# Second half's variances computed by ScalarE in the query stage, five other sums placed elsewhere, last blocks sent in halves by two queues: one transformer block on Trainium2

## The chip, the cores and the metric

The kernel runs on one core of a Trainium2 chip. A core has five engines that work side by side, each with a stream of instructions of its own that it carries out in order: TensorE (PE, matrix products, into the eight banks of the accumulator memory PSUM), VectorE (DVE), ScalarE (ACT), GpSimd (POOL) and SyncE (SP, which here only issues transfers). Sixteen DMA engines move data between device memory and the on-chip memory SBUF. Engines wait for one another by semaphores.

The metric is the device time of one execution in microseconds (us). The change is judged by the median of several runs against runs of the kernel before on the same chip.

## What is computed

The reference adds a masked cross-attention with 32 heads in 8 groups to `x`, and then a gated feed-forward block (FFN). All data are fp32; `x` is 16 x 128 x 1024, so 2048 rows of 1024.

```python
def _layernorm(x, axis=-1, eps=1e-05):
    m = jnp.mean(x, axis=axis, keepdims=True)
    v = jnp.var(x, axis=axis, keepdims=True)
    return (x - m) / jnp.sqrt(v + eps)
...
    def _L0_xattn_ref(q, k, v, w_q, w_k, w_v, w_out, mask):
...
        query = q @ w_q.T
        key = k @ w_k.T
        value = v @ w_v.T
...
        scores = jnp.einsum('bghnd,bgsd->bghns', query, key) / D_HEAD ** 0.5
        scores = jnp.where(mask, scores, jnp.finfo(scores.dtype).min)
        attention = jax.nn.softmax(scores, axis=-1)
        out = jnp.einsum('bghns,bgsd->bghnd', attention, value)
        out = out.transpose(0, 3, 1, 2, 4).reshape(b, n, D_MODEL)
        return out @ w_out.T

    def _L0_ffn_ref(x, w12, b12, w3, b3):
...
        x12 = jnp.einsum('bsk,mk->bsm', x, w12) + b12
        x1, x2 = jnp.split(x12, 2, axis=-1)
        x4 = jax.nn.silu(x1) * x2
        return jnp.einsum('bsm,nm->bsn', x4, w3) + b3
    x = x + _L0_xattn_ref(_layernorm(x, axis=-1), ctx_4096, ctx_4096, L0_xattn_w_q, L0_xattn_w_k, L0_xattn_w_v, L0_xattn_w_out, mask_SxS2_bk0)
    x = x + _L0_ffn_ref(_layernorm(x, axis=-1), L0_ffn_w12, L0_ffn_b12, L0_ffn_w3, L0_ffn_b3)
    return x
```

## The kernel before

**Products in seven instead of eight.** The large matrix products use a Strassen-like scheme: a product of 2 x 2 blocks is made from seven block products, of sums and differences of the blocks. The function `seven` runs the seven in a given order (`INNER` is 1, 5, 6, 7, 2, 3, 4) and calls a `hook(j)` after the j-th of them. One product is two instructions of 128 x 512 results per chunk; a chunk is about 0.86 us of TensorE. For the queries and for the FFN's first layer two levels are nested: an *outer* product `i` of seven is one step, and in it the *inner* products `k` of seven run. The last layer (w3) uses a scheme of 26 products, `bilinear`, for four groups `k` = 0 to 3.

The price of it is sums on the other engines. `q_outer_right(i, h, c)` makes an outer sum of the transposed `x` for product `i` (`Y`, L499, on VectorE or GpSimd); `q_inner_right(i, k)` makes from it the inner sum that product `k` needs (`Y_T`, L509, VectorE, 128 x 1024). Likewise `outer_right` (L1066 and following, on the normalised activations `xnT`) and `inner_right` (`X_T`, L1086) for the FFN. The weights' sums (`QI`, L303) run on GpSimd. Results of PSUM banks are combined on VectorE (`Q_u`, `F_u`, L287 and L290, `QUr` at L600 and L602, `M` at L1176), with a first copy by ScalarE (`Q_p`, `F_p`, L284).

**Stages**, in us of the profiled span: keys and values of the first half (0 to 65); query steps 0 to 9 (65 to 186; a step is 14 products of about 0.86 us, 12.0 us; step 3 begins at 95.4, 4 at 107.4, 5 at 119.4, 6 at 131.4, 7 at 145.6, 8 at 157.6, 9 at 169.6); attention for the first eight tiles of 128 rows (T = 0), with the remaining query steps and the second half's keys and values in between (186 to 343); attention for the other eight (T = 1) with the output projection (343 to 633); the FFN's first layer (633 to 978); w3 and the final sums (978 to 1160).

**Order.** In the query steps and in the FFN the program order of TensorE, VectorE, ScalarE, GpSimd and SP is the order in which the work is written (a manual schedule). What is to run beside the products is put into a plan: `q_at(n, j, fn, ...)` has `fn` run at hook j of query step n, `at(n, j, fn, ...)` at hook j of FFN step n. In the attention stages only TensorE's order is written by hand (`tick`, `soon` and the stream mix the attention of a tile with the products of other stages); for the other engines the scheduler of the language orders the instructions by its own estimate. Tiles come from pools: 44 buffers of 128 x 1024 (`unit`, also used by `load`), 14 of 128 x 512 (`temp`), eight banks. A buffer is passed on when its last reader is done; a load into it waits for that on its queue.

**The norm of the attention.** The layer norm's mean is taken out of the products in another way; what each tile `t` needs is 1/std. For tiles 0 to 7 (`mr[0]`) ScalarE makes the variance in the query steps: `load_xs(t)` at hook 1 of step t + 1, `q_squares(t)` at hook 2 of step t + 2 (two passes over 128 x 1024 with a sum, L626 and L628, a small negation between them, L627), then `inv_std`. For tiles 8 to 15 (`mr[1]`) VectorE does it by statistics instructions in the attention of T = 0: `mean_var` (L204 to L211) has two `bn_stats` (L208), one aggregation (L210) and a copy (L211) for a tile; loads and calls stand in the hook of `seven_round` (L733 to L736). `inv_std` (L213 to L224) is six small operations on GpSimd and two on ScalarE. The values are used from `scores` on, where `s` (L760, VectorE) scales the scores by 1/std and adds the mask; then the maximum (L763), the exponentials on ScalarE (`p`, L769), the reciprocal of the sum (L775, VectorE), the scaling of `p` (L778, GpSimd), the transposes (`pt`, TensorE L784) and their copies (L787, L789). `vt` (L426) are TensorE's transposes of the second half's values.

**Other work that the change touches.** `sums_left7(1, 0)` makes the sums of the key weights for the second half's keys, eight GpSimd additions of 128 x 256 (`A_S`, L303); the scheduler of T = 0 places them. `wo_T` and `wo` (L242) are sums of the output projection's weights by VectorE and GpSimd, `ctx_T` and `ctx` (L700) of the second half's context. `made(i, blocks, sums)` plans the four outer sums (`blocks`) and the inner ones of FFN product i; `quiet(n, c)` gives the first c of the hook positions (n, 7), (n+1, 1), (n+1, 2). For w3, `direct` (L1283 to L1288) adds a finished PSUM block or an intermediate sum into the rows `x1_in`; if it is the last term of a block of 128 x 512 (`final`), the block is sent to `out` by SP's queue.

Of the kernel before, what the change touches and what calls it, by code (L numbers as in the profile page):

```python
# [14 lines left out]
ALU = mybir.AluOpType  # L15
# [113 lines left out]
def xattn_ffn_kernel(  # L129
# [75 lines left out]
    def mean_var(xt, dst, name):  # L205
        st = small.tile([P, 2, nc.vector.BN_STATS_DIM], F32, tag="st", name=f"st_{name}")
        for h in range(2):
            nc.vector.bn_stats(st[:, h, :], xt[:, ts(h, 512)])  # L208
        mv = small.tile([P, 2], F32, tag="mv", name=f"mv_{name}")
        nc.vector.bn_aggr(mv, st)  # L210
        nc.vector.tensor_copy(dst, mv)  # L211
# [204 lines left out]
    def load_xs(t):  # L416
        xs[t] = load(x[t], [D], f"xs_{t}")

    def stats(t):
        mean_var(xs.pop(t), mr[t // NT][:, :, t % NT], f"a{t}")  # L420

    def turn_V(T, c, r, t):

        pt = bank(f"vt_{T}_{c}_{r}").rearrange("p (t k) -> p t k", t=4)
# [189 lines left out]
            *((INNER,) if n < AHEAD else ((1, 6, 5, 7, 2, 3, 4), nc.vector.tensor_copy)),  # L614
        )

    def q_stats(t):
        stats(t)
        if t % NT == NT - 1:
            inv_std(mr[t // NT], f"a{t // NT}")  # L620

    def q_squares(t):

        xt = xs.pop(t)
        less = mr[0][:, 0, t : t + 1]
        nc.scalar.activation(xt, xt, AF.Identity, accum_out=less)  # L626
        nc.scalar.mul(less, less, -1.0 / D)  # L627
        nc.scalar.activation(xt, xt, AF.Square, bias=less, accum_out=mr[0][:, 1, t : t + 1])  # L628
        if t == NT - 1:
            nc.gpsimd.tensor_scalar(mr[0][:, 1, :], mr[0][:, 1, :], 1.0 / D, None, ALU.mult)  # L630
            inv_std(mr[0], "a0")

    def q_plans():
        for n, (g, i) in enumerate(Q_STEPS):
            if i > 2:
                q_at(n - 2, 3, q_load_left, g, i)
            for e, k in enumerate((1, 5, 6, 7, 3)):
                q_at(n - 1, 3 + e if n else min(5 + e // 2, 7), q_inner_left, g, i, k)
            if i in (1, 2, 5, 3):
                q_at(n - 1, 6 if n else 7, q_hold, g, i)  # L640
            if i == 1:
                q_at(g - 1, 7, q_keep_left, g, 4)
                q_at(g - 1, 7, q_outer_left, g)
                q_at(g, 7, q_keep_left, g, 3, 6)
                q_at(g + 1, 2, q_keep_left, g, 5, 7)
                q_at(n + 1, 2, q_store, g, i, "U")
            if i == 2:
                q_at(n + 1, 2, q_gather, g, 2, "U")
                q_at(n + 2, 3, q_final, g, 2, 0, 0)
            if i == 6:  # L650
                q_at(n - 2, 4, q_fetch, g, "U")
                q_at(n + 1, 2, q_store, g, "u", "V")
            if i == 7:
                q_at(n + 1, 2, q_store, g, "u", "W")
            if i == 4:
                q_at(n, 7, q_stay, g, "u", 1)
            if i == 5:
                q_at(n + 1, 3, q_gather, g, "V", 5)
                q_at(n + 1, 3, q_gather, g, "W", 5)
                q_at(n + 1, 4, q_given, g, "W", 1)  # L660
            if i == 3:
                q_at(*((n + 1, 3) if g == 0 else (n, 7)), q_gather, g, "V", 3)
                q_at(n, 7, q_given, g, "V", 0)
        for e, (K, C) in enumerate(((0, 0), (1, 0), (1, 1), (0, 1))):
            for f, (h, c) in enumerate(((0, 0), (0, 1), (1, 1), (1, 0))):
                when = ((-1, 3 + (f + 1) // 2), (0, 1 + f), (0, 5 + f // 2), (1, 2 + f))[e]
                q_at(*when, load_xq, K, C, h, c)
        for i, hcs, ks in (
            (1, [(-1, 5)] * 4, ((-1, 6), (-1, 6), (-1, 7), (0, 1))),
            (2, [(0, 6)] * 4, ((0, 7), (1, 1), (1, 2), (1, 7))),  # L670
            (5, [(2, 1), (2, 2), (2, 7), (3, 1)], ((8, 7), (9, 1), (9, 2), (9, 7))),
            (6, [(2, 7), (3, 1), (3, 3), (3, 3)], ((3, 5), (3, 6), (3, 7), (4, 1))),
            (7, [(4, 5), (5, 1), (5, 2), (5, 5)], ((5, 2), (5, 7), (6, 1), (6, 2))),
            (4, [(6, 5), (7, 1), (7, 2), (7, 5)], ((7, 2), (7, 7), (8, 1), (8, 2))),
            (3, [(4, 4)] * 4, ((4, 4), (5, 4), (8, 4), (8, 6))),
        ):
            for when, hc in zip(hcs, ((0, 0), (0, 1), (1, 1), (1, 0))):
                q_at(*when, q_outer_right, i, *hc)
            for when, k in zip(ks, (5, 6, 7, 4)):
                q_at(*when, q_inner_right, i, k)  # L680
        for t in range(NT):
            q_at(t + 1, 1, load_xs, t)
            q_at(t + 2, 2, q_squares, t)
        for m in (0, 1, 4, 5):
            q_at(8, 1 + m, q_home, 0, m)
        q_at(11, 3, load_left7, 1)
        for j, e in ((1, 0), (1, 5), (2, 1), (4, 3)):
            q_at(12, j, lambda e=e: ctx_work[1][e][1]())
        for when, i, e in (
            ((12, 6), 5, 0), ((12, 7), 5, 1), ((13, 2), 6, 0), ((13, 4), 6, 1), ((13, 5), 7, 0), ((13, 7), 7, 1),  # L690
        ):
            q_at(*when, ctx_sum, i, e)
        q_at(13, 3, sums_left7, 1, 0)

    def ctx_sum(i, e):

# [19 lines left out]
    def seven_round(T, k, R):  # L716
        def done(rc, s, ps):
            r, c = rc
            dst = temp([512], f"vT_{T}_{c}_{r}") if k else key_home(T, c, r)
            if s is None:  # L720
                nc.scalar.copy(dst, ps)
            else:
                nc.vector.tensor_add(dst, s, ps)
            if k:
                soon(3, turn_V(T, c, r, dst))

        def hook(j):
            tick()
            if (T, k, j) == (1, 0, 4):
                sums_left7(1, 1)  # L730
            if (T, k) == (1, 0) and j < 3:
                ctx_sum(4, j - 1)
            if T == 1 and j < 5:  # L733
                load_xs(NT + 4 * k + j - 1)
            if T == 1 and j > 2 and j < 7:
                q_stats(NT + 4 * k + j - 3)  # L736
            transition(T, k, j)

        yield from seven(left7.pop((T, k)), R, f"Q7_{T}_{k}", done, hook, (1, 2, 5, 6, 7, 3, 4))
# [506 lines left out]
    made(1, [(-1, 1)] * 4, sums((-1, 2), (-1, 3), (-1, 4), (-1, 5)))  # L1246
    made(2, [(0, 1)] * 4, sums(*(quiet(n, 1)[0] for n in range(4))))
    made(3, [(4, 1)] * 4, sums(*(quiet(n, 1)[0] for n in range(4, 8))))
    made(5, quiet(7, 3) + quiet(8, 1), sums(*(quiet(n, 2)[1] for n in range(11, 15))))
    made(6, quiet(8, 3)[1:] + quiet(9, 2), sums(quiet(9, 3)[2], *quiet(10, 3)))  # L1250
    made(7, quiet(15, 2) + quiet(16, 2), sums(*quiet(17, 2), *quiet(18, 2)))
    made(4, [quiet(n, 1)[0] for n in range(11, 15)], sums(*(quiet(n, 1)[0] for n in range(19, 23))))
# [29 lines left out]
    def summed(k):  # L1282
        def direct(n, t, s, in_psum, final):  # L1283
            i, c = divmod(n, 2)
            part = x1_in[k][i][:, ts(c, 512)]
            put(nc.vector if in_psum else nc.gpsimd, part, part, "+" if s > 0 else "-", t)
            if final:
                nc.sync.dma_start(out[4 * COLS[k] + i][:, ts(c, 512)], part)  # L1288
# [124 lines left out]
```

## Time and profile before

| What | us |
| --- | --- |
| median of 3 runs | 1160.79 (1159.80, 1162.68, 1160.79) |
| the profiled execution | 1162.42 |
| its span (first to last instruction) | 1160.6 |
| TensorE busy | 1141.1 (98%) |
| VectorE busy | 848.8 (73%) |
| GpSimd busy | 653.0 (56%) |
| ScalarE busy | 395.4 (34%) |
| mean granted clock of TensorE | 0.997 of full speed |

The profiled execution lies 0.14% above the median and within the runs shown; 1.8 us of it are outside the span. In the profile, `L426` is line 426 of the kernel, `vt<-ident,vT` says that the tile `vt` is written from `ident` and `vT`, and a group's numbers are instructions, busy time and the mean of one in ns. A wait is put down to the instruction that ended it: `PE vt L426 <- ACT p L769` means that TensorE's instruction of line 426 waited for ScalarE's of line 769. The *chain of waits* goes back from the last instruction to what released it, and so on. In the windows, `PEclk` is the clock granted to TensorE, 1.00 being full speed.

### The profile page before, as it was taken

The page shows a single profiled execution, that of the slowest core. Times are in us where ns is not written, and L with a number is a line of the kernel's source. Part 1 is how long each engine was busy: PE and PEld are TensorE (multiplying, and loading weights), DVE is VectorE, ACT ScalarE, POOL GpSimd, SP SyncE. Part 2 cuts the span into 40 slices and gives each one's busy share as a digit, 9 for nine tenths or more (in the row PEclk, how much of TensorE's full clock was granted, in tenths as well). Part 3 has the DMA queues.
Part 4 walks back from the last instruction along what each step waited for, and adds up shares of the span by engine and source line. Part 5 has one row for each costly group of instructions (what it writes and reads, how often), then busy time and mean ns, then how long its engine had stood idle before and what let it go on. Part 6 is the DMA issues. An engine that isn't in the chain of part 4 may idle for free.

```text
span 1160.6 us, 13625 instructions
## 1 busy us (share of the span) xinstructions
PE 1141.1 (98%) x4232; PEld 534.2 (46%) x4232; DVE 848.8 (73%) x1179; ACT 395.4 (34%) x1429; POOL 653.0 (56%) x591
## 2 busy tenths in 40 slices
PE   9999999999989999999999999999999999999998
PEld 4444444445445554545454544444444444444443
DVE  4577988798977778778546456757777887979772
ACT  1222223657557576666361321210011022111211
POOL 5669935786567456547533359822523342648465
PEclk9999999999989999999999999999999999999999
DMA  9699674954254330332584889858734878282511
GB/s 364 251 368 348 227 265 144 211 154 153 91 200 181 128 128 37 128 128 91 200 306 165 315 334 326 237 199 259 176 121 159 212 197 272 91 270 82 173 73 73
DMA packets 70233, 227.42 MB, mean 196 GB/s; under 512 B 7824, under 2 KB 7824, under 8 KB 70160
## 3 DMA queue, kind: packets, MB, share of 16 engines
q1 hardware_dynamic: 62672, 199.81, 46.7%
q0 software_dynamic: 6624, 24.12, 11.2%
q10 hardware_dynamic: 864, 2.62, 0.6%
q8 instruction: 34, 0.56, 0.2%
q14 instruction: 39, 0.32, 0.1%
HBM read 139.49 MB, written 79.69 MB: 189 GB/s over the span
## 4 chain that ended last, share of the span: by engine, by line
PE 91%; DVE 4%; ACT 2%; issue 1%; DMA 1%; POOL 1%; SPq 0%; ACTq 0%; POOLq 0%; DVEq 0%
PE F_b L199 28%; PE Q_b L199 21%; PE O_b L199 15%; PE G_b L199 15%; PE pt L784 4%; PE s L751 3%; PE o L799 2%; ACT p L769 2%; PE xt L899 1%; DVE ctx_T L700 1%; DVE s L760 0%; DVE xnT L1066 0%; DVE Y_T L509 0%; DMA xnr<-xn_dram 0%; PE vt L426 0%
## 5 line engine op out<-in xcount | busy, mean ns | idle before, releaser
L769 ACT ACTIVATE p<-s,nmax 128x128 f32<-128x128 f32 x512 | 181.8, 406 | 125.7 <-DVE nmax L763 114.8
L778 POOL TENSOR_TENSOR p<-p,inv 128x512 f32<-128x512 f32 x128 | 136.4, 1098 | 138.4 <-DVE inv L775 121.1
L199 PE MATMUL F_b<-X_T,L 128*128 128x512 f32 x304 | 135.7, 592 | 0.0
L769 ACT ACTIVATION_READ_ACCUMULATOR p<-s,nmax 128x1 f32 x512 | 125.5, 245 | 0.0
L199 PE MATMUL G_b<-w_R,A_L 128*128 128x512 f32 x256 | 114.5, 592 | 0.0
L760 DVE SCALAR_TENSOR_TENSOR s<-s,mr,drop 128x512 f32<-128x512 f32 x128 | 90.3, 750 | 28.8 <-PE s L751 28.6
L784 PEld LDWEIGHTS pt<-ident,p 128*128 128x128 f32 x512 | 63.6, 142 | 70.0 <-issue 63.5
L199 PEld LDWEIGHTS F_b<-X_T,L 128*128 128x128 f32 x304 | 57.4, 190 | 70.8 <-issue 68.6
L763 DVE TENSOR_REDUCE nmax<-s 128x4 f32<-128x512 f32 x128 | 81.7, 679 | 0.0
L284 ACT COPY F_p<-F_b 128x512 f32<-128x512 f32 x28 | 16.4, 586 | 188.3 <-PE F_b L199 188.3
L784 PE MATMUL pt<-ident,p 128*128 128x128 f32 x512 | 77.3, 274 | 1.5 <-issue 1.5
L303 POOL TENSOR_TENSOR x<-x,G_n 128x512 f32<-128x512 f32 x36 | 52.8, 1491 | 46.3 <-DVE G_n L366 29.4
L384 ACT COPY G_c<-G_b 128x512 f32<-128x512 f32 x52 | 30.5, 586 | 140.7 <-PE G_b L199 137.3
L199 PEld LDWEIGHTS G_b<-w_R,A_L 128*128 128x128 f32 x256 | 48.6, 190 | 61.3 <-issue 59.3
L1176 DVE TENSOR_TENSOR M<-F_u,F_b 128x512 f32<-128x512 f32 x57 | 39.0, 685 | 46.3 <-PE F_b L199 42.8
L303 POOL TENSOR_TENSOR x<-x,G_c 128x512 f32<-128x512 f32 x36 | 54.8, 1538 | 31.9 <-DMA x<-x_dram 13.0
L199 PE MATMUL Q_b<-Y_T,QI 128*128 128x512 f32 x136 | 62.4, 594 | 1.9 <-DVE Y_T L509 1.9
L199 PE MATMUL O_b<-wo_T,O_S 128*128 128x512 f32 x128 | 63.3, 603 | 0.0
L199 PE MATMUL O_b<-wo,O_S 128*128 128x512 f32 x128 | 62.5, 602 | 0.0
L199 PE MATMUL F_b<-xnT,L 128*128 128x512 f32 x128 | 60.9, 593 | 0.0
L199 PE MATMUL O_b<-wo,OTr 128*128 128x512 f32 x112 | 56.0, 603 | 0.0
L287 DVE TENSOR_TENSOR F_u<-F_b,F_p 128x512 f32<-128x512 f32 x28 | 19.3, 691 | 45.2 <-PE F_b L199 41.5
(244 smaller groups left out, 2265.9 us busy)
## 6 DMA issues: line engine op xcount, KB each, us to landing
w<-in_w_dram SPq DMA_DIRECT2D x36, 512.0 KB, 6.3
xq<-in_xT_dram SPq DMA_DIRECT2D x16, 512.0 KB, 9.8
xs<-in_x_dram SPq DMA_DIRECT2D x16, 512.0 KB, 6.8
xp<-in_x_dram SPq DMA_DIRECT2D x16, 512.0 KB, 6.6
x_dram<-xp SPq DMA_DIRECT2D x16, 512.0 KB, 2.8
xn_dram<-xn SPq DMA_DIRECT2D x16, 512.0 KB, 2.9
xnr<-xn_dram SPq DMA_DIRECT2D x16, 512.0 KB, 5.7
h<-hT_dram SPq DMA_DIRECT2D x16, 512.0 KB, 6.0
```

Source lines behind the costliest of these rows:

```text
L199: nc.tensor.matmul(ps, lhsT, rhs, start=start and i == 0, stop=stop and i == len(pairs) - 1, skip_group_check=True,)
L287: nc.vector.tensor_add(u1, banks[6], p1)
L303: (eng.tensor_add if op == "+" else eng.tensor_sub)(out, a, b)
L384: nc.scalar.copy(t, ps)
L751: nc.tensor.matmul(ps[gl][:, j, :], QT[T, gh * HPG + j][rows, c, toks], KT[T, c][rows, gh, toks], start=True, stop=True,)
L760: nc.vector.scalar_tensor_tensor(s, s, rstd, drop.unsqueeze(1).to_broadcast([P, HPG, S]), ALU.mult, ALU.add,)
L763: nc.vector.tensor_reduce(nmax[:, e], s, AX.X, ALU.max, negate=True)
L769: nc.scalar.activation(p[:, j, :], ps[gl][:, j, :], AF.Exp, bias=nmax[:, e, j : j + 1], accum_out=total[:, e, j : j + 1],)
L778: nc.gpsimd.tensor_mul(p, p, inv[:, e].unsqueeze(2).to_broadcast([P, HPG, S]))
L784: nc.tensor.transpose(pt[:, j, :], p[:, j, :], ident)
L799: nc.tensor.matmul(o[ds(gl * DH, DH), :, :], V[T, c][:, i, ts(gh * GL + gl, DH)], pTs[gl], start=True, stop=True,)
L1176: nc.vector.tensor_add(dst, s, ps)
```

## The change

It has five parts. (1) The second half's variances: `stats`, `q_stats` and their loads in the hook of `seven_round` go; `q_squares` serves both halves. For tile 8 + t the load stands at hook 3 (even t) or 5 (odd t) of query step 3 + t//2, and the squares one step and one hook later. The last calls `inv_std(mr[1])`. (2) Inner sums of the queries: that of k = 6 for outer product 7 from hook 7 to hook 4 of step 5; for outer product 3, k = 6 from (5, 4) to (8, 3), k = 7 from (8, 4) to (8, 5), k = 4 from (8, 6) to (9, 4). (3) `sums_left7(1, 0)` from (13, 3) to (12, 2). (4) Two of the four outer sums of FFN product 5: from (7, 7), (8, 1), (8, 2), (8, 7) to (7, 7), (8, 1), (8, 7), (9, 1). (5) In the last group of w3 (`k == 3`) a block that ends with a PSUM term (there are four) is added in two halves of 256 columns, and each is sent as soon as it is added, the first by SP's queue, the second by ScalarE's.

TensorE's instructions and their order are the same in both kernels. VectorE has 16 `bn_stats`, 8 aggregations and 8 copies less and 4 additions more (each of half the size); ScalarE has 24 activations and 4 transfers more. In the scheduled attention stage of T = 0, GpSimd's eight `A_S` sums come ahead of the `p` scaling of tile 1, one of two `wo` sums of GpSimd comes between the two pairs of `p` scalings that it used to follow, and one `wo_T` sum of VectorE takes the place of two `bn_stats` some 8 us earlier.

```diff
--- before.py
+++ after.py
@@ -416,9 +416,6 @@
     def load_xs(t):
         xs[t] = load(x[t], [D], f"xs_{t}")
 
-    def stats(t):
-        mean_var(xs.pop(t), mr[t // NT][:, :, t % NT], f"a{t}")
-
     def turn_V(T, c, r, t):
 
         pt = bank(f"vt_{T}_{c}_{r}").rearrange("p (t k) -> p t k", t=4)
@@ -614,21 +611,17 @@
             *((INNER,) if n < AHEAD else ((1, 6, 5, 7, 2, 3, 4), nc.vector.tensor_copy)),
         )
 
-    def q_stats(t):
-        stats(t)
-        if t % NT == NT - 1:
-            inv_std(mr[t // NT], f"a{t // NT}")
-
     def q_squares(t):
 
         xt = xs.pop(t)
-        less = mr[0][:, 0, t : t + 1]
+        T, e = divmod(t, NT)
+        less = mr[T][:, 0, e : e + 1]
         nc.scalar.activation(xt, xt, AF.Identity, accum_out=less)
         nc.scalar.mul(less, less, -1.0 / D)
-        nc.scalar.activation(xt, xt, AF.Square, bias=less, accum_out=mr[0][:, 1, t : t + 1])
-        if t == NT - 1:
-            nc.gpsimd.tensor_scalar(mr[0][:, 1, :], mr[0][:, 1, :], 1.0 / D, None, ALU.mult)
-            inv_std(mr[0], "a0")
+        nc.scalar.activation(xt, xt, AF.Square, bias=less, accum_out=mr[T][:, 1, e : e + 1])
+        if e == NT - 1:
+            nc.gpsimd.tensor_scalar(mr[T][:, 1, :], mr[T][:, 1, :], 1.0 / D, None, ALU.mult)
+            inv_std(mr[T], f"a{T}")
 
     def q_plans():
         for n, (g, i) in enumerate(Q_STEPS):
@@ -670,9 +663,9 @@
             (2, [(0, 6)] * 4, ((0, 7), (1, 1), (1, 2), (1, 7))),
             (5, [(2, 1), (2, 2), (2, 7), (3, 1)], ((8, 7), (9, 1), (9, 2), (9, 7))),
             (6, [(2, 7), (3, 1), (3, 3), (3, 3)], ((3, 5), (3, 6), (3, 7), (4, 1))),
-            (7, [(4, 5), (5, 1), (5, 2), (5, 5)], ((5, 2), (5, 7), (6, 1), (6, 2))),
+            (7, [(4, 5), (5, 1), (5, 2), (5, 5)], ((5, 2), (5, 4), (6, 1), (6, 2))),
             (4, [(6, 5), (7, 1), (7, 2), (7, 5)], ((7, 2), (7, 7), (8, 1), (8, 2))),
-            (3, [(4, 4)] * 4, ((4, 4), (5, 4), (8, 4), (8, 6))),
+            (3, [(4, 4)] * 4, ((4, 4), (8, 3), (8, 5), (9, 4))),
         ):
             for when, hc in zip(hcs, ((0, 0), (0, 1), (1, 1), (1, 0))):
                 q_at(*when, q_outer_right, i, *hc)
@@ -681,6 +674,8 @@
         for t in range(NT):
             q_at(t + 1, 1, load_xs, t)
             q_at(t + 2, 2, q_squares, t)
+            q_at(3 + t // 2, 3 + t % 2 * 2, load_xs, NT + t)
+            q_at(4 + t // 2, 4 + t % 2 * 2, q_squares, NT + t)
         for m in (0, 1, 4, 5):
             q_at(8, 1 + m, q_home, 0, m)
         q_at(11, 3, load_left7, 1)
@@ -690,7 +685,7 @@
             ((12, 6), 5, 0), ((12, 7), 5, 1), ((13, 2), 6, 0), ((13, 4), 6, 1), ((13, 5), 7, 0), ((13, 7), 7, 1),
         ):
             q_at(*when, ctx_sum, i, e)
-        q_at(13, 3, sums_left7, 1, 0)
+        q_at(12, 2, sums_left7, 1, 0)
 
     def ctx_sum(i, e):
 
@@ -730,10 +725,6 @@
                 sums_left7(1, 1)
             if (T, k) == (1, 0) and j < 3:
                 ctx_sum(4, j - 1)
-            if T == 1 and j < 5:
-                load_xs(NT + 4 * k + j - 1)
-            if T == 1 and j > 2 and j < 7:
-                q_stats(NT + 4 * k + j - 3)
             transition(T, k, j)
 
         yield from seven(left7.pop((T, k)), R, f"Q7_{T}_{k}", done, hook, (1, 2, 5, 6, 7, 3, 4))
@@ -1246,7 +1237,7 @@
     made(1, [(-1, 1)] * 4, sums((-1, 2), (-1, 3), (-1, 4), (-1, 5)))
     made(2, [(0, 1)] * 4, sums(*(quiet(n, 1)[0] for n in range(4))))
     made(3, [(4, 1)] * 4, sums(*(quiet(n, 1)[0] for n in range(4, 8))))
-    made(5, quiet(7, 3) + quiet(8, 1), sums(*(quiet(n, 2)[1] for n in range(11, 15))))
+    made(5, quiet(7, 2) + quiet(8, 2), sums(*(quiet(n, 2)[1] for n in range(11, 15))))
     made(6, quiet(8, 3)[1:] + quiet(9, 2), sums(quiet(9, 3)[2], *quiet(10, 3)))
     made(7, quiet(15, 2) + quiet(16, 2), sums(*quiet(17, 2), *quiet(18, 2)))
     made(4, [quiet(n, 1)[0] for n in range(11, 15)], sums(*(quiet(n, 1)[0] for n in range(19, 23))))
@@ -1283,6 +1274,11 @@
         def direct(n, t, s, in_psum, final):
             i, c = divmod(n, 2)
             part = x1_in[k][i][:, ts(c, 512)]
+            if final and in_psum and k == 3:
+                for h, queue in enumerate((nc.sync, nc.scalar)):
+                    put(nc.vector, part[:, ts(h, 256)], part[:, ts(h, 256)], "+" if s > 0 else "-", t[:, ts(h, 256)])
+                    queue.dma_start(out[4 * COLS[k] + i][:, ds(512 * c + 256 * h, 256)], part[:, ts(h, 256)])
+                return
             put(nc.vector if in_psum else nc.gpsimd, part, part, "+" if s > 0 else "-", t)
             if final:
                 nc.sync.dma_start(out[4 * COLS[k] + i][:, ts(c, 512)], part)
```

## The prediction

> **What bounds the kernel now.** I read the page's busy times first, then TensorE's waits, the chain of waits around each, and last the windows.
>
> ```profile
> PE 1141.1 (98%) x4232; PEld 534.2 (46%) x4232; DVE 848.8 (73%) x1179; ACT 395.4 (34%) x1429; POOL 653.0 (56%) x591
> ...
> PE 91%; DVE 4%; ACT 2%; issue 1%; DMA 1%; POOL 1%; SPq 0%; ACTq 0%; POOLq 0%; DVEq 0%
> ```
>
> TensorE works 1141.1 of 1160.6 us. The edits leave its instructions and their order alone, so a gain can only come out of the other 19.5 us or out of time at a lowered clock. TensorE's own waits (total, times, longest) show where:
>
> ```profile
> PE vt L426 <- ACT p L769: 5.3, 1, 5.3
> PE Q_b L199 <- DVE Y_T L509: 1.9, 1, 1.9
> ...
> PE F_b L199 <- DVE M L1176: 1.2, 1, 1.2
> ...
> PE s L751 <- DVE QM L606: 0.9, 1, 0.9
> ```
>
> The longest, followed back through the chain (start, us, what):
>
> ```profile
> 313.20 1.15 DVE st_a L208 x2
> 314.35 1.14 DVE wo_T L242
> 315.49 0.12 DVE mv_a L210
> 315.61 1.86 DVE wo_T L242
> 317.47 2.23 DVE mr L211
> 319.70 0.59 DVE st_a L208
> 320.30 1.32 DVE s L760 x2
> ...
> 323.88 1.11 PE vt L426 x4
> ```
>
> TensorE ran out of work at 318.53 and resumed at 323.88. ScalarE's exponentials are what it waits for, but they were waiting for `s` at 320.30, and VectorE had spent 313.20 to 320.30 on the second half's variances (L208, L210, L211) and two sums `wo_T`. The idle time also lowered the clock (windows: length, busy us of PE, PEld, DVE, ACT, POOL, then PEclk):
>
> ```profile
> 315.00:320.00 5.00, 3.53 (x36) 1.27 (x28) 5.00 (x5) 0.00 (x0) 5.00 (x3) 1.00 0.00 0
> 320.00:325.00 5.00, 1.12 (x5) 1.12 (x6) 5.00 (x9) 2.68 (x16) 1.98 (x1) 0.62 0.01 2
> 325.00:330.00 5.00, 5.00 (x16) 2.62 (x16) 3.61 (x9) 4.72 (x23) 3.32 (x5) 0.70 0.75 220
> ```
>
> At half clock a mean of 0.62 means 0.76 of the 5 us at half, and 0.70 means 0.60: 3.8 + 3.0 = 6.8 us, from about 321.2 to 328.0. TensorE worked 4.1 us of it (323.88 to 328.0) at half speed, so it lost 2.05 us beside the idle 5.34. The wait costs 7.4 us.
>
> **The change, part by part.**
>
> *Variances.* Out go 16 `bn_stats` (0.68 us each), 8 aggregations (0.20) and 8 copies (0.18, one 2.31): 10.9 + 1.6 + 3.6 = 16.1 us of VectorE. Around the wait it loses 313.20–314.35, 315.49–315.61 and 317.47–320.30. What is late next is the pair of `wo_T` sums. Alone they take 1.22 each: `s` starts at 313.2 + 2.44 = 315.6. Beside a GpSimd sum of two SBUF operands the same VectorE form takes 1.74 to 3.37 (L509), and GpSimd here has `p` (1.04, 2.02) and its own `wo` sums (3.33, 2.34), one of which now comes earlier: 313.2 + 1.94 + 3.3 = 318.4 at worst. I take the middle, 317.0. From `s` to `vt` it was 323.88 − 320.22 = 3.66, so `vt` starts at 320.7 (319.3 to 322.1) against 318.53: a wait of 2.2 (0.8 to 3.5). The clock fell 321.2 − 318.53 = 2.7 us into the wait, and the 1.91 us wait at 135 left it at 1.00, so 2.2 us should leave it whole. Gain 5.34 − 2.2 + 2.05 = **5.2**; from 5.34 − 3.5 = 1.8 (clock still lost) to 5.34 − 0.8 + 2.05 = 6.6.
>
> The Trainium skill, "TensorE: Matmul & The Clock Gate", Part 1, says that the clock falls after an idle window of about 3.4 us that runs free of the program. By that rule a wait between 2.7 and 3.4 us might keep its clock, and the gain would be up to 2 us larger than the row makes it there; for a wait of 2.2 both give 5.2.
>
> The work goes to ScalarE: 8 × (1.06 + 0.19 + 0.20 + 1.15 + 0.19 = 2.79) = 22.3 us in query steps 4 to 7, two tiles a step, which had one. ScalarE's busy time there is:
>
> ```profile
> 119.40:131.40 12.00, 12.00 (x29) 5.32 (x28) 11.83 (x15) 3.08 (x6) 10.90 (x7) 1.00 0.73 271
> 131.40:145.60 14.20, 12.29 (x30) 5.22 (x29) 13.39 (x13) 3.08 (x6) 14.12 (x8) 1.00 0.42 153
> 145.60:157.60 12.00, 12.00 (x29) 5.31 (x28) 10.10 (x11) 3.08 (x6) 9.63 (x9) 1.00 0.60 218
> ```
>
> 3.08 + 5.6 = 8.7 of 12.0 fits, so nothing on the path; uncovered it would be 22.3. Eight loads of 512 KB move with it, from 250–330 to steps 3 to 6. SP issues them in order, and DMA's share in steps 2 to 4 is over 1.0 (1.02, 1.05, 1.04 in windows cut by step). Loads behind them are `QL`, needed by GpSimd's `QI`: in step 4 `QL` was issued at 109.89, landed at 120.12, and `QI` took it at 121.6. `QI` is 3 us or more ahead of TensorE. A buffer of 44 is owned by somebody else until that work ends, so some of the loads wait on SP for a square or a write (a write of `Q_dram` landed at 117.74), but SP idles from 112.8 to 122.2. I take 0; the other end stands as a rival. GpSimd's six small operations of `inv_std` come at 156 to 159, ahead of `QI` that is needed at 166: 0.
>
> *Query sums.* The wait at 135.02:
>
> ```profile
> 132.35 1.14 DVE QUr L602
> 133.48 3.31 DVE Y_T L509
> ```
>
> `Y_T` (k=6 of i=7) is made just ahead of its product, with GpSimd's `xq` sum (2.81 us from 132.89) beside it. Three hooks earlier it starts near 127.9 and takes the 1.74 us of the `Y_T` that stood there. Behind it k=7's sum (1.74 at 136.71) starts at 133.41 and must be done by 136.6: alone at 134.6, beside `xq` at 136.8, so 0 to 0.3 us remain. Gain 1.91 minus 0.2 = **1.7** (1.0 if the earlier sum delays step 5's `QUr` chain, to 1.9). Steps 8 and 9 take the three moved sums of i=3, 1.2 each; in step 9 VectorE has idles of 0.25 + 1.03 + 0.30 = 1.6 ahead of the chain that starts at 183.17 (`Y_T`, then `s`): 0, at most 1.2 without that cover.
>
> *Left sums.* Eight GpSimd sums (5.65 us) move from 241–249 to 221.8, where GpSimd idles till 225.16. They hold `p` of 225.16 back by 2.4 us, which TensorE turns only at 236. They free GpSimd at 241–245.7, where `p` waited; then `ctx` of 249.08 is over sooner and `ctx_T`, 4.00 us at 252.51 beside two-operand GpSimd work, comes nearer its 1.22, and `QM` behind it at 256.44 ends the wait of 0.94. I take half of it, **0.5** (0 to 0.94 + 0.45 for the small wait at 249.48).
>
> *FFN sums.* Ahead of the wait at 746.48:
>
> ```profile
> 736.71 1.14 DVE X_T L1086
> 737.85 3.35 DVE xnT L1066 x2
> 741.20 0.11 issue
> 741.31 1.74 DVE xnT L1066
> ...
> 746.96 0.69 DVE M L1176
> ```
>
> Three `xnT` sums hold `F_u` to 742.98; with two it starts at 741.3, 1.7 earlier, more than the wait of 1.21. The other two are then both in step 9, where `F_u` started at 754.93, right after `X` sums. They were 1.26 at 750.31 and one more of 1.26 to 1.74 joins; of that VectorE's idle in 748.2–750.3 covers most. Gain **1.2** (0.2 if 1 us of it comes back there, to 1.21).
>
> *Tail.* The last add took 0.69 (128x512), issue at 1157.36, landing 1159.40, end 1160.62. Halves take 0.42 each (128x256): the second ends 0.15 later, both transfers are half as large. 256 KB is a small part of the 2.04 us, since four such transfers just before land 0.6 to 1.2 us apart. Gain **0.1** (−0.3 to +0.4).
>
> The Trainium skill, "DMA: Bandwidth & Descriptors", in "Issuing engines are not separate DMA queues" and "Anatomy of one DMA", speaks against this edit: queues share the 16 engines, and about 2 us of a transfer is fixed. By it the halves would bring nothing but the issue time, 0; by the rows 0.1.
>
> *Sum:* 5.2 + 1.7 + 0.5 + 1.2 + 0.1 = 8.7 us. The profiled execution took 1162.4 (span 1160.6 and 1.8 around it), so the same execution would take 1153.7. The median of the runs shown, 1160.8, is 1.6 lower: **1152.1**. All upper ends together give 6.6 + 1.9 + 1.4 + 1.2 + 0.4 = 11.5, thus 1149.3.
>
> **Rivals.**
>
> *`wo_T` takes the place of the statistics* (0.18). GpSimd's work of 313–322 stays beside `wo_T`, both run near 3 us, and `s` comes at 318.4: that part brings 1.8 only. For it: `mr`'s copy of two numbers took 2.31 while GpSimd's `wo` sum ran from 316.35. Against: `wo_T` took 1.22 and 1.94 in just this neighbourhood. 8.7 − 3.4 = 5.3: 1155.5.
>
> *The moved work stalls where it is put* (0.13): besides, FFN's wait moves to 755, the left sums hold `p` back until it shows, `Y_T` keeps 0.9. All lower ends: 1.8 + 1.0 + 0 + 0.2 − 0.3 = 2.7: 1158.1. Also what it would be if the change did not do what it says at 318. Against: each of the three places has the idle time given above.
>
> *Slower: ScalarE waits in order for a late load* (0.11). The square stands ahead of the next step's copy `Q_p` in ScalarE's order. If its tile has not landed, `Q_p` and the two products' banks behind it wait. A tile has 12.9 us from its hook to its square (a step and one hook of 0.86). A load that waits 5.9 us on SP (the longest wait of that queue for TensorE at 95–119) and takes 13.8 (the longest there, issued at 96.22) is 6.8 late. TensorE goes on for 8 banks × 0.86 = 6.9 minus one being filled and the copy (0.86 + 0.59), 5.4 us. It decides from there: 6.8 costs 1.4 once; 7.6 us late in each of four steps, 4 × 2.2 = 8.8, eats up the gain; 9 us late, with waits past the 2.7 us and one clock loss, is 4 × 3.6 + 2.05 = 16.4: 1168.5. For it: DMA at 1.05, and eight more transfers. Against: its share falls to 0.73 and 0.42 in steps 4 and 5, where most of the new loads are.
>
> **How the numbers follow.** Likeliest 0.58, at 1152.1, with an own range of 1149.3 to 1155.5; rivals 0.18, 0.13 and 0.11. The range takes in the first three cases with the bounds of their parts, and leaves out little but the slower rival: 1148.5 to 1160.0. The runs shown lie 2.9 us apart, 0.25%, so 0.3% or 3.5 us is about what is told from no change. Faster than 1157.3: the first two cases, 0.76. Within: the third, 0.13. Slower than 1164.3: 0.11, the last.
>
> **What would show it.** Right: no wait of TensorE over 3 us after 300, PEclk 1.00 at 320–330, `s` at L760 before 318.5; no wait for `Y_T` near 135; none for `M` near 746 or 757; ScalarE busy near 8.7 us in steps 4 to 7 and TensorE 12.0 of 12.0 in each. Wrong: `vt` still waiting 3.5 us or more behind `wo_T`; a wait of Q_b for Q_u or `QI` between 95 and 186; a new wait near 236 for `p`.

## The result: slower by 0.4%

| Kernel | median, us | runs | ratio to the kernel before, 95% interval |
| --- | --- | --- | --- |
| before | 1160.09 | 10 (1158.75 to 1162.68) | |
| changed | 1165.38 | 10 (1163.11 to 1167.85) | 1.0040 [1.0028, 1.0052] |

5.3 us were lost where 8.7 were forecast as a gain. The page of the changed kernel's profiled execution (1164.81 us, span 1163.0), its engines' busy times:

```profile
PE 1141.6 (98%) x4232; PEld 533.5 (46%) x4232; DVE 838.9 (72%) x1151; ACT 415.2 (36%) x1469; POOL 652.8 (56%) x592
```

VectorE has 9.9 us less (16.1 had been counted out), ScalarE 19.8 more, and TensorE's work is what it was. So the time went into waits again. TensorE's waits in the changed kernel (total, times, longest; line numbers have moved, L423 is `vt`, L760 the exponentials, L775 the transposes `pt`, L1167 `M`):

```profile
PE Q_b L199 <- POOL QI L303: 4.4, 2, 4.1
PE vt L423 <- ACT p L760: 2.4, 1, 2.4
PE pt L775 <- ACT p L760: 1.6, 1, 1.6
...
PE Q_b L199 <- DVE xq L506: 1.4, 1, 1.4
...
PE F_b L199 <- DVE M L1167: 0.4, 1, 0.4
```

The waits that were aimed at did shrink: `vt` from 5.3 to 2.4, the one for `Y_T` from 1.9 to 0.3, `M` from 1.2 to 0.4. Three new ones have come: `QI` (4.1 at 127.5), `xq` (1.4 at 141.9) and `pt` (1.6 at 242.7). Two of these are among the signs of being wrong that the prediction named: a wait for `QI` between 95 and 186, and one for `p`, which it put near 236.

How far the same TensorE instruction is behind the kernel before, from the start times of the two traces, gives each place its price (us; negative is earlier):

| Place (us in the changed kernel) | what | difference |
| --- | --- | --- |
| start to 124 | run-to-run, see the last section | −0.75 |
| 124 to 135 | wait for `QI`, and a stretch at half clock behind it | +5.8 |
| 140 | `Y_T` no longer waited for | −2.0 |
| 142 to 166 | `xq` and `Y_T` late behind the first wait | +2.0 |
| 243 to 251 | `pt`, and `Q_b` and `s` behind it | +3.3 |
| 264 | `s` no longer waits for `QM` | −1.2 |
| 325 to 352 | `vt`: shorter wait, one stretch at half clock instead of two | −3.5 |
| 750 | FFN (0.8 of it the wait for `M`) | −1.0 |
| end | tail, from the end of the last product | −0.3 |
| sum | | +2.4 |

The sum is that of the two spans (1163.0 and 1160.6). The medians lie further apart because the profiled execution of the kernel before was 2.3 above its median and that of the changed kernel 0.6 below.

Where the `QI` wait comes from is seen on GpSimd. Its timeline in the changed kernel (start, duration, line, operation, and in brackets the idle time before and what ended it):

```profile
107.36 0.86 POOL L570 DMA_DIRECT2D QM<-QU_dram  x1 [0.63 <-DVE QM L603]
118.90 0.72 POOL L303 TENSOR_TENSOR QI<-QL 128x256 f32<-128x256 f32 x1 [10.68 <-DMA Q_dram<-QM]
...
124.41 4.66 POOL L496 TENSOR_TENSOR xq<-xq,xq 128x1024 f32<-128x1024 f32 x2
129.04 1.70 POOL L303 TENSOR_TENSOR QI<-QL 128x256 f32<-128x256 f32 x1
130.82 0.73 POOL L303 TENSOR_TENSOR QI<-QI,QL 128x256 f32<-128x256 f32 x1
```

GpSimd stands still for 10.7 us, and not for an input: it waits until the transfer `Q_dram<-QM` has landed. It *writes* `QI`, and the buffer that `QI` got is the one that `QM` is still being sent out of. Behind that, all of GpSimd's order is late; TensorE goes on at 131.6, when the two `QI` sums of 129.04 and 130.82 are done. In the kernel before, GpSimd's waits for `QI` from 92 to 134 were these:

```profile
POOL QI L303 <- DMA QL<-QS_dram: 1.0, 1, 1.0
```

The wait also cost clock; windows of the changed kernel (length, busy PE, PEld, DVE, ACT, POOL, then PEclk, DMA share, GB/s):

```profile
124.00:129.00 5.00, 3.51 (x8) 1.25 (x7) 2.21 (x1) 4.20 (x10) 5.00 (x3) 1.00 0.99 375
129.00:134.00 5.00, 2.37 (x3) 1.18 (x4) 4.93 (x5) 0.00 (x0) 4.92 (x5) 0.71 1.02 382
```

ScalarE, which had got the squares, idles from 129 to 134: it isn't what is late. DMA is full in both windows, so two explanations were open: the buffer, or the eight more transfers.

### The profile page after: what moved, and what is told of

Its sections match the earlier page's. It is cut to its first block, busy times and chain, and to the rows that moved or that the text cites. A ratio compares the mean times of both kernels' runs of the same rounds, so it can differ in the third digit from the quotient of the medians.

```text
span 1163.0 us, 13650 instructions
## 1 busy us (share of the span) xinstructions
PE 1141.6 (98%) x4232; PEld 533.5 (46%) x4232; DVE 838.9 (72%) x1151; ACT 415.2 (36%) x1469; POOL 652.8 (56%) x592
## 4 chain that ended last, share of the span: by engine, by line
PE 87%; DVE 5%; DMA 3%; ACT 2%; issue 2%; POOL 1%; DVEq 0%; ACTq 0%; POOLq 0%; SPq 0%
PE F_b L199 28%; PE Q_b L199 18%; PE G_b L199 15%; PE O_b L199 15%; PE pt L775 4%; PE s L742 3%; PE o L790 2%; ACT p L760 2%; DMA Q_dram<-QM 1%; DVE s L751 1%; DMA xs<-in_x_dram 1%; DVE nmax L754 1%; DVE xp L870 1%; PE xt L890 1%; DVE ctx_T L695 1%
## 5 line engine op out<-in xcount | busy, mean ns | idle before, releaser
L760 ACT ACTIVATE p<-s,nmax 128x128 f32<-128x128 f32 x512 | 181.8, 406 | 124.4 <-DVE nmax L754 108.5
L769 POOL TENSOR_TENSOR p<-p,inv 128x512 f32<-128x512 f32 x128 | 139.0, 1124 | 136.3 <-DVE inv L766 117.9
L760 ACT ACTIVATION_READ_ACCUMULATOR p<-s,nmax 128x1 f32 x512 | 125.3, 245 | 0.0
L775 PEld LDWEIGHTS pt<-ident,p 128*128 128x128 f32 x512 | 63.8, 142 | 71.8 <-issue 62.9
L775 PE MATMUL pt<-ident,p 128*128 128x128 f32 x512 | 77.6, 275 | 3.1 <-ACT p L760 1.6
L1167 DVE TENSOR_TENSOR M<-F_u,F_b 128x512 f32<-128x512 f32 x57 | 39.0, 685 | 45.7 <-PE F_b L199 41.9
L303 POOL TENSOR_TENSOR x<-x,G_c 128x512 f32<-128x512 f32 x36 | 52.0, 1462 | 31.7 <-DMA x<-x_dram 12.9
```

The source lines that it names most:

```text
L303: (eng.tensor_add if op == "+" else eng.tensor_sub)(out, a, b)
L760: nc.scalar.activation(p[:, j, :], ps[gl][:, j, :], AF.Exp, bias=nmax[:, e, j : j + 1], accum_out=total[:, e, j : j + 1],)
L769: nc.gpsimd.tensor_mul(p, p, inv[:, e].unsqueeze(2).to_broadcast([P, HPG, S]))
L775: nc.tensor.transpose(pt[:, j, :], p[:, j, :], ident)
```

## The experiments

Which buffer a tile gets is fixed when the program is built: the pool hands out one of 44 by what it reckons to be free first. The addresses in the compiled programs show which tile had the buffer before; the waits in the profiles agree with them. For the second group's `QI` of product 6 (query step 5):

| Kernel | the `QI` buffer's last owner | tile 11's load (SP) |
| --- | --- | --- |
| before | a query weight, long done | none |
| changed | `QM`, being written to `Q_dram` | another `QM`, being written |
| `qi_same_buffer` | `QM`, being written to `Q_dram` | another `QM`, being written |
| `qi_free_buffer` | tile 8, until its squares | tile 9 |
| `qi_free_sp_waits` | tile 2, until its squares | `QM`, being written |
| `late_two_steps`, `late_three_steps`, `traffic` | a query weight, long done | none in step 4 |

**The first part alone** (`var_only`): the kernel before with the loads and squares of part 1 as the change has them, parts 2 to 5 left out.

```diff
+            q_at(3 + t // 2, 3 + t % 2 * 2, load_xs, NT + t)
+            q_at(4 + t // 2, 4 + t % 2 * 2, q_squares, NT + t)
...
-            if T == 1 and j < 5:
-                load_xs(NT + 4 * k + j - 1)
-            if T == 1 and j > 2 and j < 7:
-                q_stats(NT + 4 * k + j - 3)
```

> The kernel before with the first part alone: tiles 8 to 15's variances by ScalarE, their eight loads in query steps 3 to 6. Theory (buffers): the eight extra tiles change which of the 44 buffers the weight sum QI of step 5 gets; it gets one whose write to device memory (Q_dram) is still under way, GpSimd stands about 10 us at 108 to 119 and TensorE waits for QI near 125 to 131 (about 4 us and a clock window at half), while the wait for vt falls to 2 to 3 us: 1161 to 1165 us, slower than 1160.1. Rival (this part is harmless, the loss of the changed kernel comes from the other parts): about 1155, no wait for QI before 186.

1165.91 us, 1.0045 [1.0031, 1.0058]. The wait for `QI` is there (4.1 us at 126.4) and the `vt` wait is 2.43: the part alone costs as much as the whole change (1.0040), and 0.9 us more than the upper end of what was expected.

**All but the first part** (`no_var`): the changed kernel with the statistics back on VectorE.

```diff
-            q_at(3 + t // 2, 3 + t % 2 * 2, load_xs, NT + t)
-            q_at(4 + t // 2, 4 + t % 2 * 2, q_squares, NT + t)
...
+            if T == 1 and j < 5:
+                load_xs(NT + 4 * k + j - 1)
+            if T == 1 and j > 2 and j < 7:
+                q_stats(NT + 4 * k + j - 3)
```

> The changed kernel without its first part: the second half's variances again by VectorE statistics in the attention of T = 0, the other four parts kept. Theory (buffers): no wait for QI near 127; the Y_T wait of 1.9 us at 135 gone, the FFN wait of 1.2 mostly gone, the tail 0.3 shorter, the left sums at 222 cost 2 to 3 us near 237 and give 1.2 back near 257, the vt wait of 5 us is back: 1157.5 to 1160. Rival (the loss is in the other parts): 1163 or more.

1160.32 us beside 1161.07, 0.9992 [0.9983, 1.0001], 0.3 us above the range that was expected. No wait for `QI`; the `pt` wait of 1.57 us is there at 235.6, as in the changed kernel, and the `vt` wait is 5.35. The first part makes the loss, but the other four together bring nothing clear of it either.

**The buffer, with all else kept** (`qi_free_buffer`, and as a control `qi_same_buffer`): one load a hook earlier, or a hook later; the squares of that tile at the same hook in both (the comment gives the control's hook).

```diff
-            q_at(3 + t // 2, 3 + t % 2 * 2, load_xs, NT + t)
-            q_at(4 + t // 2, 4 + t % 2 * 2, q_squares, NT + t)
+            q_at(*((3, 4) if t == 1 else (3 + t // 2, 3 + t % 2 * 2)), load_xs, NT + t)   # control: (3, 6)
+            q_at(*((4, 6) if t == 1 else (4 + t // 2, 4 + t % 2 * 2)), q_squares, NT + t)
```

> The changed kernel with one load moved by one hook: tile 9's from hook 5 to hook 4 of step 3, its squares at hook 6 of step 4 in place of 4 would be the same place as now but two hooks later. All loads, squares and transfers remain; only the buffers fall differently: QI of step 5 gets tile 8's buffer, tile 11's load that of tile 9, so neither GpSimd nor SP waits for a write of Q_dram. Theory (buffers): the 10.7 us wait of GpSimd at 108 goes, TensorE's 4 us wait for QI near 127 and the half clock there with it: 1158 to 1160.5. Rivals (ScalarE's squares in order, or eight more transfers in a full DMA): unchanged, 1164 to 1166.

> The control: the changed kernel with tile 9's load moved one hook the other way (from hook 5 to hook 6 of step 3) and its squares at hook 6 of step 4. QI of step 5 keeps the buffer with the write of Q_dram under way. Theory (buffers): GpSimd waits 10 us or so at 108 as in the changed kernel, TensorE about 4 us near 127: 1164 to 1166.5. If only moving that load helped, for whatever other reason, it would be near 1159.

1161.15 us, 0.9999 [0.9987, 1.0011], and 1164.82, 1.0029 [1.0017, 1.0040], in the same comparison. The eight loads, the squares and the bytes are the same in both. GpSimd's waits for `QI` from 92 to 134, first in the control, then with the other buffer:

```profile
POOL QI L303 <- DMA Q_dram<-QM: 10.7, 1, 10.7
```

```profile
POOL QI L303 <- ACT xs L621: 5.6, 1, 5.6
```

TensorE's longest waits from 92 to 186, in the same order:

```profile
PE Q_b L199 <- POOL QI L303: 4.5, 2, 4.1
```

```profile
PE Q_b L199 <- DVE Q_u L290: 3.2, 2, 2.2
```

With a buffer of tile 8 `QI` still waits, now for that tile's squares, and TensorE still waits 2.2 us at 127.5, for `Q_u`, in a chain that goes back to a load of `QL` that landed at 121; so the median is 0.65 us above the range that was expected. The control has TensorE's 4.1 us for `QI`.

**GpSimd's wait or SP's** (`qi_free_sp_waits`). In the changed kernel SP's queue waits for a write of `Q_dram` too (8.3 us, for tile 11's load), with `QL`, `QV` and `Q_dram` behind it. Here tile 9 is loaded at hook 4 of step 4, and only SP's wait is left:

```diff
+            q_at(*((4, 4) if t == 1 else (3 + t // 2, 3 + t % 2 * 2)), load_xs, NT + t)
+            q_at(*((5, 2) if t == 1 else (4 + t // 2, 4 + t % 2 * 2)), q_squares, NT + t)
```

> The changed kernel with tile 9's load at hook 4 of step 4 (in place of hook 5 of step 3) and its squares at hook 2 of step 5. The buffers fall so that QI of step 5 gets that of tile 2, whose squares are done early, while tile 11's load still gets one behind a write of Q_dram: GpSimd's wait of 10 us at 108 goes, SP's wait of 8 us (with QL, QV and Q_dram transfers behind it in its order) stays. If GpSimd's wait makes TensorE's 4 us near 127: 1159 to 1161.5. If SP's wait does, by the loads and writes behind it: 1164 to 1166.

1159.69 us beside 1160.69, 0.9994 [0.9983, 1.0005]. The waits of GpSimd and of SP's queue from 92 to 134, and TensorE's longest from 92 to 186:

```profile
POOL QI L303 <- ACT xs L621: 3.1, 1, 3.1
```

```profile
SPq L193 <- DMA Q_dram<-QM: 4.9, 1, 4.9
```

```profile
PE Q_b L199 <- DVE Q_u L290: 1.5, 2, 1.1
```

SP waits for the write, 4.9 us of it, and TensorE's wait near 128 is 1.1 us. Followed from 124 to 190 us, TensorE's instructions fall 6.1 us further behind in the control than here. So it was GpSimd's wait that cost. SP's is shorter here than in the changed kernel, so this run alone does not exclude a small share of it; but `qi_free_buffer`, where SP waits for no write of `Q_dram`, is no faster.

**The transfers alone** (`traffic`): the kernel before with eight copies of 512 KB added on SP's queue at the hooks of the new loads, from device memory to device memory, so that no buffer is taken and nothing waits for them. They are extra work; the result does not use them.

```diff
+    def q_traffic(t):
+        nc.sync.dma_start(tc.dram_tile([P, D], F32, name=f"spare_{t}"), x[t])
...
+            q_at(3 + t // 2, 3 + t % 2 * 2, q_traffic, NT + t)
```

> The kernel before with eight copies of 512 KB from device memory to device memory added on SP's queue at the eight hooks of the new loads (steps 3 to 6): the same bytes at the same places, but no buffer in SBUF and nothing that waits for them; the output is not touched. Theory (buffers, not traffic): within 1.5 us of the kernel before, 1160 to 1162, no wait for QI over 1 us. Rival (eight more transfers in a DMA that is already full): 4 us or more slower, 1164 and above, with QL and QM landing 3 us or more later than in the kernel before.

1160.78 us beside 1161.35, 0.9996 [0.9987, 1.0004]. GpSimd waits a little longer for `QL`:

```profile
POOL QI L303 <- DMA QL<-QS_dram: 2.9, 2, 1.9
```

That is 2.9 instead of 1.0 us. From 95 to 160 the loads of `QL` take 6.8 us to land and those of `QM` 10.3 (medians), 5.3 and 9.8 in the kernel before, and TensorE does not wait for `QI` at all; it waits 1.3 us for `xq` and 0.6 for `Y_T`, together the 1.9 of the kernel before. The full DMA is not the cause by itself.

**The left sums** (`no_left7`): the changed kernel with its third part undone.

```diff
-        q_at(12, 2, sums_left7, 1, 0)
+        q_at(13, 3, sums_left7, 1, 0)
```

> The changed kernel with its third part undone: sums_left7(1, 0) back from (12, 2) to (13, 3). Theory from the traces so far: ahead of p's scaling the eight GpSimd sums run beside VectorE's ctx_T (5.45 us there instead of 1.2) and make VectorE, then ScalarE's p late; TensorE waits 1.6 + 0.8 near 243 and gets back 1.2 near 257. Undone: these two waits go, the small one of 0.9 near 257 returns: about 2 us (up to 3.7 where a clock window was lost) less than the changed kernel, 1162 to 1164. Rival (the prediction's: that part gives 0.5): 1165.5 to 1166.

1163.56 us, 1.0023 [1.0015, 1.0032] where the changed kernel has 1.0040 [1.0028, 1.0052]: about 2 us less, though the two intervals just meet. VectorE's `ctx_T` in the timeline of the changed kernel, then in this one:

```profile
234.64 5.45 DVE L695 TENSOR_TENSOR ctx_T<-ctx,ctx 128x1024 f32<-128x1024 f32 x1
```

```profile
235.79 1.22 DVE L695 TENSOR_TENSOR ctx_T<-ctx,ctx 128x1024 f32<-128x1024 f32 x1
```

GpSimd's work beside it in the changed kernel:

```profile
234.44 2.53 POOL L769 TENSOR_TENSOR p<-p,inv 128x512 f32<-128x512 f32 x2
236.43 1.21 POOL L303 TENSOR_TENSOR QI<-QI,QL 128x256 f32<-128x256 f32 x1
237.12 1.20 POOL L303 TENSOR_TENSOR QI<-QL 128x256 f32<-128x256 f32 x1
237.80 1.19 POOL L303 TENSOR_TENSOR QI<-QL,QI 128x256 f32<-128x256 f32 x1
```

GpSimd, late behind the eight sums, works on `p` and `QI` without a gap from 231.8 to 239.0, and `ctx_T` takes 4.2 us longer beside it. `QM`, `s`, the exponentials and `pt` follow, in this order. The waits of 1.58 and 0.77 us that the changed kernel has at 242.7 and 245.0 are gone here.

**The loads later** (`late_two_steps`, `late_three_steps`): part 3 left out, and the loads and squares where the buffers that come round are free (the comments give the step in the first of the two).

```diff
-            q_at(3 + t // 2, 3 + t % 2 * 2, load_xs, NT + t)
-            q_at(4 + t // 2, 4 + t % 2 * 2, q_squares, NT + t)
+            q_at(6 + t // 2, 3 + t % 2 * 2, load_xs, NT + t)      # late_two_steps: 5
+            q_at(7 + t // 2, 4 + t % 2 * 2, q_squares, NT + t)    # late_two_steps: 6
...
-        q_at(12, 2, sums_left7, 1, 0)
+        q_at(13, 3, sums_left7, 1, 0)
```

> The changed kernel with the third part undone and the eight loads two query steps later: hooks 3 and 5 of steps 5 to 8, squares one step and one hook later (steps 6 to 9). QI of step 5 then has the buffer it has in the kernel before, of a weight that was done long ago; only one load (tile 10) takes a buffer behind a write. Theory (buffers): no wait of GpSimd near 108, none of TensorE for QI near 127, the wait for Y_T gone; the vt wait about 2.4, FFN 0.4: 1153.5 to 1156.5. Rival (ScalarE's share): the squares now stand in steps 6 to 9, two per step as before, and would cost the same there: 1162 or more.

> As the one before, with loads in steps 6 to 9 and squares in steps 7 to 10; tiles 14 and 15's squares then lie in the attention stage where the scheduler places them beside the exponentials. Theory (buffers): 1153.5 to 1157; the last two tiles on ScalarE (2.8 us each) may cost up to 1 us in the attention near 190. Rival (ScalarE's share): 1162 or more.

1155.00 us, 0.9946 [0.9933, 0.9959], and 1154.11 us, 0.9936 [0.9923, 0.9950], beside 1161.35. Both beat both kernels; the second by 7.2 us over the kernel before. TensorE's waits in it:

```profile
PE vt L423 <- ACT p L760: 2.4, 1, 2.4
...
PE s L742 <- DVE QM L603: 0.9, 1, 0.9
...
PE F_b L199 <- DVE M L1167: 0.4, 1, 0.4
```

ScalarE's 22.3 us of squares are all in it, and no wait of TensorE between 92 and 185 is over 0.2 us (one of 0.8 us for `Q_p` follows at 185.9). So the squares as such were not the trouble.

**What each half of it brings** (`parts_2_4_5`, without part 1 and 3; `late_alone`, part 1 with the late loads, without the others). The edits against the kernel before are, for the first:

```diff
-            (7, [(4, 5), (5, 1), (5, 2), (5, 5)], ((5, 2), (5, 7), (6, 1), (6, 2))),
+            (7, [(4, 5), (5, 1), (5, 2), (5, 5)], ((5, 2), (5, 4), (6, 1), (6, 2))),
...
-            (3, [(4, 4)] * 4, ((4, 4), (5, 4), (8, 4), (8, 6))),
+            (3, [(4, 4)] * 4, ((4, 4), (8, 3), (8, 5), (9, 4))),
...
-    made(5, quiet(7, 3) + quiet(8, 1), sums(*(quiet(n, 2)[1] for n in range(11, 15))))
+    made(5, quiet(7, 2) + quiet(8, 2), sums(*(quiet(n, 2)[1] for n in range(11, 15))))
...
+            if final and in_psum and k == 3:
+                for h, queue in enumerate((nc.sync, nc.scalar)):
...
```

and for the second that of `var_only`, with 6 and 7 in place of 3 and 4.

> The kernel before with the query sums, the FFN sums and the halves of the tail alone (parts 2, 4 and 5; no variances by ScalarE, the left sums at their old place). By the traces so far: the Y_T wait of 1.9 us at 135 goes and 0.2 to 0.3 come behind it, FFN's wait of 1.2 becomes 0.4, the tail is 0.3 shorter: 2.8 us less than the kernel before, 1158 to 1159 beside 1161. If these parts only looked well in single traces: within 1 us of the kernel before.

> The kernel before with the first part alone, its loads in steps 6 to 9 and its squares in steps 7 to 10. By the traces so far: the wait for vt falls from 5.3 to 2.4 us and one clock window at half of two goes (2.9 + 1.7 = 4.6 at most, less where the last window stays), and about 0.7 is lost near 190: 4 us less than the kernel before, 1156.5 to 1158 beside 1161. With parts 2, 4 and 5 (2.8 us) that is the 7 us which all four brought together. If ScalarE's share cost something in these steps: 1159 or more.

1156.63 us, 0.9964 [0.9951, 0.9976], and 1158.18 us, 0.9977 [0.9966, 0.9988], beside 1160.92. The first gave more than was expected (4.3 us; its interval reaches from 2.8 to 5.7), the second less (2.7 us, from 1.4 to 3.9); together they are the 7 us of `late_three_steps`. Why the split is not 2.8 and 4 is settled only in part. The wait of 0.94 us for `QM` at 256 is missing in both profiles, some 1.3 us in each, while `late_three_steps` has it; the profile of `late_alone` has a wait of 1.4 us for `Q_p` at 188.6 and one of 1.3 us for `xnr` at 586, both 0.2 in the kernel before; waits of 0.8 and 1.1 us stand at these places in `late_three_steps` too.

## Why the prediction was wrong, step by step

**The step that failed** is this one in the part on the variances: "A buffer of 44 is owned by somebody else until that work ends, so some of the loads wait on SP for a square or a write … I take 0". It followed buffers only for the eight new loads. But each new tile can shift the buffer of *any* tile after it, and GpSimd's outputs come from the same pool. What the runs showed in its place: `QI` got a buffer that was still being written out, GpSimd stood 10.7 us, and that ate the "3 us or more" by which `QI` was said to be ahead of TensorE. It cost 5.8 us by the traces up to 135 and another 2.0 up to 166. With the same eight loads, one of them moved so that `QI` gets another buffer, the loss against the kernel before is gone (1161.15 and 1159.69 against 1164.82).

**The slower rival** had the right sign and the right steps by luck, for its mechanism was the wrong one. It let ScalarE wait in its order for a late load. In the changed kernel ScalarE's waits from 95 to 160 are for TensorE's products and once for `QI`, never for a load. The argument against that rival, DMA's falling share, was about something that did not decide.

**Left sums.** "They hold `p` of 225.16 back by 2.4 us, which TensorE turns only at 236" counted the delay and its cover, but not what runs beside the late work: the two-operand sums of GpSimd now fell on VectorE's `ctx_T`. Forecast +0.5, measured about −2 where it is undone in the changed kernel. A second pair shows it more clearly: `no_var` and `parts_2_4_5` differ in this part alone, and it makes 0.9992 [0.9983, 1.0001] of 0.9964 [0.9951, 0.9976], 3.3 us. The 0.94 us wait for `QM`, half of which was put down as the gain, is itself not always there: it is missing in the profiles of `traffic`, `var_only`, `parts_2_4_5` and `late_alone`, which have the sums at the old place.

**`vt`** went as worked out but for the clock: by the traces it gave 3.5 of the 5.2 us that were forecast. In the chain of the changed kernel:

```profile
320.15 2.48 DVE wo_T L242 x2
322.62 1.62 issue
324.25 1.41 DVE s L751 x2
...
327.92 0.66 PE vt L423 x4
```

The `wo_T` pair, beside GpSimd, takes 2.28 and 2.06 us and `s` starts 4.2 us after the first; 3.8 was taken. The wait is 2.44 where 2.2 was forecast. What was off is "2.2 us should leave it whole": a stretch at half clock follows all the same, one instead of two. The last section shows that the length of a wait does not decide this.

**`Y_T`** was right: the wait is gone and 0.2 to 0.3 us come behind it where GpSimd is not late (`no_var`, `late_three_steps`). **FFN** was right in mechanism and too large: 0.8 us for 1.2. `F_u` does come sooner, but the gated product behind it (L1150; L1159 in the kernel before, where it took 2.74 us) takes 3.42 beside a GpSimd sum of 128x1024 and gives part of it back; nothing of it came back in step 9. **The tail** gave 0.3 for 0.1: from TensorE's last product to the end of the span 4.08 us before, 3.74 after, and 3.73 to 3.75 in the other profiles with that part. The transfers got no shorter: from issue to landing 2.0 us for 256 KB before, 2.1 and 1.9 for 128 KB on the two queues (medians). No run separates the halves from the second queue.

**The sum** without the failed step and the left sums was 8.2 us. The version that has neither trouble measured 7.2. That these are so near is partly luck: part 1, with the late loads, gave 2.7 us alone where 5.2 were forecast for it, and parts 2, 4 and 5 gave 4.3 for 3.0.

## What to carry to other kernels

When a tile is added to a shared pool, follow who owned the buffer of each later tile, outputs of every engine included: an extra load that fits on its own queue can make another engine wait for a write that it has nothing to do with. Where such a wait appears, the profile names a transfer that is no input of the waiting instruction; move the new tile to where the buffers that come round have long been free, and the work itself may cost nothing. An idle stretch of GpSimd is free only if what it pushes back doesn't fall beside VectorE's sums of two SBUF operands.

## What the runs showed of the hardware

**The clock is set window by window, and the idle time within a window decides.** The clock records of the thirteen profiles know full and half clock alone. Each stretch at half clock within a span is 3.41 us or twice that, and each stretch at full clock is a whole number of 3.413 us (122.88 is 36 of them, 310.61 is 91). So the windows can be laid through a profile from its first change of clock. In thirteen such windows at full clock TensorE's matrix products left 2.04 us or more idle, and half clock followed each time; with 1.84 us or less it never did. Between them lie 1.88 and 1.93 (half clock followed) and 1.96 (it did not). The length of a wait is not what counts, since it may lie in one window or be shared by two. The `vt` wait of 2.4 us lowered the clock in five of nine profiles (the changed kernel, where 2.25 us of it lay in one window, `var_only`, `no_left7` and both late ones); in `late_alone` it was split into 1.75 and 0.7 and did not. One of 1.88 us at 749 in `var_only` lay whole in a window and did; one of 3.2 us at 139 was split into 1.35 and 1.83 and did not. The wait of 5.35 us lowered it twice over in all four profiles that have it. The Trainium skill, "TensorE: Matmul & The Clock Gate", Part 1, has a window of 3413 ns that runs free of the program, and these lengths agree. It has the clock fall after an idle window of about 3.4 us; here 2.04 us within one were enough, and the measurement decides. The reading of the prediction (2.7 us into a wait) took for a length what was the place of the window.

**The start moves the time by 2 us and more.** TensorE reached full clock 3.9 us after the start of the span in `late_three_steps` and 10.6 us in the kernel before, the ends of what the thirteen profiles show, and 12 us into the span the same instruction came 2.4 us earlier in the first. Executions of one kernel differ by 1.6 to 6.7 us here, so single profiles were compared stage by stage and not by their ends.

**VectorE and GpSimd take turns.** A 128x1024 sum of two SBUF operands is 1.22 us on VectorE alone; beside GpSimd's work it was 2.28 and 2.06 (`wo_T`), 3.36 (`Y_T` at 126.8) and 5.45 (`ctx_T`), while GpSimd's `p` went from 1.04 to 2.02. In the profiles of both kernels each such sum (`Y_T`, `X_T`, `ctx_T`, `wo_T`) that took over 2 us ended 1.08 or 1.09 us after a GpSimd operation did, and that is nearly the whole 1.22: it was done after GpSimd's, not beside it. `ctx_T` sat out five GpSimd operations that followed one another.
